# A decoder block with long convolutions on one core: part of the filter transform and five inverse transforms split by steps modulo 4, and two additions moved from TensorE to GpSimd

## The chip, the cores and the metric

The kernel runs on one core of a Trainium2 chip. The metric is the device time of one execution in microseconds, as the median of several executions; lower is better. A profile is one execution taken by the hardware profiler: it records every instruction of the five engines. The text calls them PE (TensorE, matrix multiplication; PEld is its weight loading, which overlaps), DVE (VectorE), ACT (ScalarE), POOL (GpSimd) and SP (SyncE, which only issues transfers here).

## The reference

One decoder block over `x` of shape (4, 1024, 256): a Hyena operator, cross attention to 64 context positions, and a feed-forward layer with ternary weights, each followed by a residual and a layer norm. Everything is float32.

```python
def hyena(u):                                  # per batch, L = 1024, D = 256
    res = depthwise_conv3((u @ w_in.T + b_in).T, conv_w, conv_b)   # 3 * D channels
    x0, x1, v = res.split(3)
    h = hyena_filter(L, D, ...)                # 2 filters per channel, each of length L
    for n in range(2):                         # two orders
        y = irfft(rfft(v, 2 * L) * rfft(h[n], 2 * L))[:L]
        v = y * (x0, x1)[n]
    return v.T @ w_out.T + b_out

x = layernorm(x + hyena(x))
x = layernorm(x + cross_attention(x, ctx))     # 16 heads of 16, 64 keys, output bias b_out
x = layernorm(x + bitlinear_ffn(x))            # 256 -> 1024 gate and up -> 256, quantised activations
```

What matters here is the long convolution, done by matrices in place of a fast transform; the output bias of the attention; and the quantised inner layer, whose rounded values are held with an offset.

## The kernel before

**Long convolution.** The work is cut in eight units: four batches times two halves of 128 channels. A unit runs `stage_j` (three projections with a width-3 convolution, done on ACT and by accumulating transfers that GpSimd issues), `stage_tv` and `stage_tx` (eight 128 x 128 PE transposes each, in `turned`), and then for each of the two orders a data transform `stage_f`, a product with the filter's transform `stage_p`, and an inverse transform `stage_i0` or `stage_i1`. `stage_i1` ends with a multiply by `x1` into `v2s`, and `stage_o` (one for each batch) does the output projection, the residual and the layer norm.

The transforms are plain matrix products against cosine and sine tables `fw` (forward) and `gi_` (inverse), 512 x 512 each. Even and odd steps are already transformed apart: each half needs matrices of half the size, and DVE joins the two results by one sum and one difference (`stage_f`, lines 655 and 656). So a data transform is 16 float32 matmuls of 128 x 128 weights against 256 columns, and so is an inverse transform: for each of four output blocks, four matmuls that sum over cosines and sines (lines 713 and 736). The profile counts a float32 matmul as two passes with a weight load each. In `stage_i0` the table is the weights and the data are the 256 columns; in `stage_i1` the data are the weights and the table the columns.

The filters are transformed once (`filters`, line 523): the eight blocks `hsb` of 128 steps x 512 (two filters, 256 channels) go through 32 matmuls of 512 columns, `ha`, one group of four for each (`dl`, `cs`, `kt`). ACT copies half of each result to `hospace`, DVE writes sum and difference into `hf`, and two large multiply-adds over `hf` finish it. PE, DVE and ACT queue in program order here, with four PSUM buffers of 1024 columns (`big1`).

**From unit 6 on** (line 836) the instructions are not issued as written. `Engines` holds every call as a `Step`; `plan` (line 248) then lists them engine by engine, greedily: among the steps whose inputs are ready, or nearly so within `SLACK`, it takes the one with the lowest rank, which is its place `at` plus an `OFFSET` for its stage. `cost` (line 108) holds the planner's assumed durations. So the last two units, the rest of the convolutions (`rest`, line 874) and the 32 attention and feed-forward tiles of 128 tokens are mixed into one order, which is then kept.

**Attention and feed-forward, per tile.** `att_s` (scores and their maxima on DVE, split into parts on GpSimd), `att_e` (scores again, less the maxima, and the exponential on ACT), `att_v` (values and denominators, on PE with small weights), `att_o` (output projection, residual, norm), `ffn_x` (quantise, transpose), `ffn_h` (gate and up, their product, its maximum, quantise), `ffn_d` (down projection), `ffn_o` (norm and store).

Two details that the change touches. In `att_o`, the output bias enters as a matmul of ones against the bias row `brow` that opens the PSUM sum (line 1162). In `ffn_h`, GpSimd copies the low halves of the rounded values to `h16` (line 1213), which SP's transposing transfer turns to `hT`; these halves carry an offset of 1536 (`HALF`). `ffn_d` sums eight matmuls against `wd_q` and takes the offset out with a ninth, `neg16` against `wd_s`, the sum of the weights (line 1223), which `sum_wd` prepares once on GpSimd (line 1003).

`norm` (line 1148) is statistics on DVE, a reciprocal root by GpSimd's power, and a scaling on DVE.

Of the kernel before, what the change touches and what calls it, by code (L numbers as in the profile page):

```python
# [20 lines left out]
INNER = 1024  # L21
EPS = 1e-5
MAGIC = 12582912.0

# [60 lines left out]
class Step:  # L85
# [22 lines left out]
    def cost(self):  # L108

        n = self.n  # L110
        if self.dma:
            if "transpose" in self.what:
                return 1.25, 2.2
            if self.engine == "POOL":
                return 1.3, 5.0
            return 0.45, 2.0 + self.out.nbytes() / 90e3
        if self.engine == "PE":
            lhs, rhs = self.ins[0], self.ins[1]
            if self.what == "transpose":
                return (0.11 if self.out.dtype == FP else 0.056), 0.2  # L120
            one = 0.002 + rhs.free_size() * (2 if rhs.dtype == FP else 1) / 2400
            one = 2 * max(one, 0.112) if rhs.dtype == FP else one

            return (one / 4 if self.mode else one), 0.2
        if self.engine == "DVE":
            if self.what == "reciprocal" and n > 8:
                return 0.27, 0.17
            if self.what == "scalar_tensor_tensor":
                return 0.065 + n / 900, 0.17
            return 0.065 + n / 960, 0.17  # L130
        if self.engine == "ACT":
            return 0.1 + n * 0.00098, 0.15
        if self.what == "tensor_copy":
            return 0.1 + n * 0.00096, 0.06
        return 0.52 + n * 0.001 * (n > 64), 0.06

# [163 lines left out]
def follow(steps, before, order):  # L300
# [6 lines left out]

SLACK = {"PE": 0.00, "DVE": 0.10, "ACT": 0.72, "POOL": 0.0, "SP": 0.0}
TABLE_RANK = 2.87
OFFSET = dict(  # L310
    att_q=-0.91, att_e=-2.18, att_s=-3.90, att_v=-1.58, att_o=-0.51, ffn_x=-0.32, ffn_h=-1.21, ffn_d=2.05, ffn_o=8.51, rest=-1.48
)
# [3 lines left out]
def decoder_kernel(  # L316
# [81 lines left out]
    def layernorm(r, dst, name):  # L398
# [54 lines left out]
    if True:  # L453
# [69 lines left out]
        def filters():  # L523

            hsb = [spare[4 + t // 2][:, t % 2 * 512 : t % 2 * 512 + 512] for t in range(8)]
            for t in (0, 1, 4, 5, 2, 3, 6, 7):
# [3 lines left out]
                tt_(hsb[t], hsb[t], fdb[:, 1, :], ALU.add)  # L530
            n = 0
            for dl in range(2):
                for cs in range(2):
                    for kt in range(2):
                        m = (2 * cs + kt) * P
                        ha = big1(f"ha{dl}_{cs}_{kt}")
                        for par in range(2):
                            for mt in range(2):
                                mm(
                                    ha[:, par * 512 : par * 512 + 512],  # L540
                                    fw[:, 2 * par + mt, m : m + P],
                                    hsb[4 * par + 2 * dl + mt],
                                    start=mt == 0,
                                    stop=mt == 1,
                                )
                        ho = hospace[:, n % 4]
                        n += 1
                        nc.scalar.copy(ho, ha[:, 512:1024])
                        for st, op in ((0, ALU.add), (1, ALU.subtract)):
                            f = slice(st * 256 + kt * P, st * 256 + kt * P + P)  # L550
                            tt_(
                                hf[:, :, dl, cs, f],
                                ha[:, 0:512].rearrange("p (n d) -> p n d", d=P),
                                ho.rearrange("p (n d) -> p n d", d=P),
                                op,
                            )
            for cs in range(2):
                stt(
                    hf[:, :, 1, cs, :],
                    hf[:, :, 0, 1 - cs, :],  # L560
                    pv[:, C_SG + cs : C_SG + cs + 1],
                    hf[:, :, 1, cs, :],
                    ALU.mult,
                    ALU.add,
                )

# [35 lines left out]
        def turned(u, src, dst, name):  # L602

            ps = big1(f"tr{name}_{u}")
            for par in range(2):
                for j in range(2):
                    for mt in range(2):
                        c, o = (4 * par + 2 * j + mt) * P, (4 * par + 2 * mt + j) * P
                        nc.tensor.transpose(ps[:, o : o + P], src[:, c : c + P], ident)
            nc.scalar.copy(dst, ps)  # L610
# [22 lines left out]
        def stage_f(u, n):  # L633
# [3 lines left out]
            vf = r_vf().rearrange("p (c s f) -> p c s f", c=2, s=2)  # L637
            s["vf"] = vf
            for cs in range(2):
                ps = big1(f"f{u}_{n}_{cs}")  # L640
# [17 lines left out]
        def stage_p(u, n, half):  # L658
# [41 lines left out]
            tt_(q2[:, 0], q1[:, :, 0, :], q1[:, :, 1, :], ALU.add)  # L700
            tt_(q2[:, 1], q1[:, :, 0, :], q1[:, :, 1, :], ALU.subtract)

        def stage_i0(u, *parts):
# [6 lines left out]
            for i in parts or range(4):  # L710
                par, mt = i // 2, i % 2
                o = i * 256
                for m in range(4):
                    mm(
                        ps[:, o : o + 256],
                        gi_[:, m, par * 256 + mt * P : par * 256 + mt * P + P],
                        y[:, par, m // 2, (m % 2) * 256 : (m % 2) * 256 + 256],
                        start=m == 0,
                        stop=m == 3,
                    )  # L720
# [4 lines left out]
        def stage_i1(u):  # L725
# [7 lines left out]
            for par in range(2):  # L733
                for j in range(2):
                    o = (2 * par + j) * 256
                    for m in range(4):
                        c = (m % 2) * 256 + j * P
                        mm(
                            ps[:, o : o + 256],
                            y[:, par, m // 2, c : c + P],  # L740
                            gi_[:, m, par * 256 : par * 256 + 256],
                            start=m == 0,
                            stop=m == 3,
                        )
            tt_(v2s[b][:, dh, :], ps, s["x1"], ALU.mult)

# [252 lines left out]
    r_hT = Ring(*parts(hfree[3][:, 512:2048], 8 * P, F16))  # L999

    wd_s, neg16 = q0h[0][:, 512:640].bitcast(F16), q0h[0][:, 640:704].bitcast(F16)

    def sum_wd():
        nc.gpsimd.memset(neg16, -HALF)
        part = q0h[0][:, 0:512].bitcast(F16)
        w = wd_q.rearrange("p k f -> p (k f)")
        nc.gpsimd.tensor_tensor(part, w[:, 0:1024], w[:, 1024:2048], ALU.add)
        nc.gpsimd.tensor_tensor(part[:, 0:512], part[:, 0:512], part[:, 512:1024], ALU.add)
        nc.gpsimd.tensor_tensor(wd_s, part[:, 0:256], part[:, 256:512], ALU.add)


    kb = {}
# [135 lines left out]
    def norm(r, dst, name):  # L1148
# [6 lines left out]
        nc.gpsimd.tensor_tensor(rs, ve, mhalf[:, 0:1], ALU.pow)  # L1155
        ts_(dst, r, mv[:, 0:1], rs, ALU.subtract, ALU.mult)
# [36 lines left out]
    def ffn_h(g, t):  # L1193
# [61 lines left out]
    while done_d < NT:  # L1255
# [16 lines left out]
        if i == 7:  # L1272
            nc.at, nc.stage = i, "rest"
            sum_wd()
        n = 0 if i < 8 else 2 if i % 4 == 3 else 1
# [18 lines left out]
def _constants():  # L1294
# [9 lines left out]
    even_odd = np.arange(L).reshape(L // 2, 2).T.reshape(L)  # L1304
    t = np.linspace(0.0, 1.0, L, dtype=np.float32)[even_odd]
    bands = np.arange(33, dtype=np.float32)
# [76 lines left out]
```

## Time and profile before

| what | us |
|---|---|
| median of 3 executions | 723.73 |
| lowest and highest of them | 722.44, 726.07 |
| the profiled execution | 723.07 |
| its span, first to last instruction | 721.3 |

| stretch of the span | from | to |
|---|---|---|
| loads, filter basis, first projections | 0 | 33.4 |
| filter transforms (`ha`) | 33.4 | 60.9 |
| convolutions, issued as written | 60.9 | 309.5 |
| planner's order: last convolutions with the first attention tiles | 309.5 | 479 |
| attention with feed-forward | 479 | 690 |
| last tiles run out | 690 | 721.3 |

How to read it: busy time adds up the records of an engine's instructions in a stretch; an engine busy for the whole of it sets its length. Matmuls are pipelined, so a record is longer than the time until the next one starts, and the pace is read from a row of many. The chain of waits goes back from the last instruction, at each step to whatever released it. "issue" is time in which the engine waited for nothing that the profile shows.

### The profile page before, as it was taken

What the parts mean: (1) busy time and instruction counts of PE and PEld (TensorE: products, weight loads), DVE (VectorE), ACT (ScalarE), POOL (GpSimd) and SP (SyncE); (2) the same over time, 40 slices, a digit from 0 to 9 for tenths busy, and PEclk for the clock granted to TensorE, in tenths of its full rate; (3) what the DMA queues carried; (4) which work ended last, traced back from release to release, by engine and by line L of the source; (5) the groups of instructions that cost most, each with busy time, mean ns of one, the idle gap of its engine ahead of it and who ended that gap; (6) DMA issues with size and microseconds to landing.
All of it is one profiled execution on the core that took longest, in us unless ns stands there. A gap on an engine that the chain in (4) does not pass through costs nothing.

```text
span 721.3 us, 12520 instructions
## 1 busy us (share of the span) xinstructions
PE 680.3 (94%) x4920; PEld 472.6 (66%) x4950; DVE 604.2 (84%) x1125; ACT 371.2 (51%) x522; POOL 192.0 (27%) x347
## 2 busy tenths in 40 slices
PE   5999899999999999989999989999999999999973
PEld 2346487878687786867868856866666666566632
DVE  4636759999989999689866986587999898999996
ACT  5512535163461526306322112349898889788861
POOL 1210212012121221214101034123344334343443
PEclk9999999999999999999999999999999999999996
DMA  8853655457370654705830100000222223222133
GB/s 294 169 107 118 141 93 91 84 102 133 59 161 15 140 94 75 129 1 100 185 117 2 58 1 1 2 2 16 53 59 54 53 45 67 39 60 60 38 79 96
DMA packets 65296, 57.61 MB, mean 80 GB/s; under 512 B 38516, under 2 KB 49396, under 8 KB 65238
## 3 DMA queue, kind: packets, MB, share of 16 engines
q0 software_dynamic: 13056, 25.17, 20.6%
q1 hardware_dynamic: 47612, 27.84, 14.8%
q10 hardware_dynamic: 4570, 3.81, 1.8%
q8 instruction: 39, 0.64, 0.4%
q14 instruction: 19, 0.16, 0.1%
HBM read 17.47 MB, written 4.19 MB: 30 GB/s over the span
## 4 chain that ended last, share of the span: by engine, by line
PE 75%; DVE 16%; issue 2%; POOL 2%; DMA 2%; ACT 1%; ACTq 0%; POOLq 0%; DVEq 0%; SPq 0%
PE ps_t L82 37%; PE f L61 12%; PE i L61 10%; PE pj L61 9%; PE ha L61 4%; DVE q L82 3%; DVE small_t L82 3%; PE o L61 2%; DVE x1sp L82 1%; DMA w_in<-in_w_inT 1%; DVE q L61 1%; DVE xt L82 1%; DVE x1sp L61 1%; DVE x1c L82 1%; DVE ln_t L82 1%
## 5 line engine op out<-in xcount | busy, mean ns | idle before, releaser
L82 PE MATMUL ps_t<-hf 128*128 128x256 f16 (+1 forms) x482 | 101.9, 332 | 11.1 <-DMA hf<-vf 3.3
L61 PE MATMUL f<-vt,fw 128*128 128x256 f32 x384 | 84.9, 379 | 1.1 <-ACT vt L61 1.1
L61 POOL DMA_DIRECT2D xc<-tap x28 | 33.9, 1245 | 193.2 <-ACT tap L61 119.5
L82 PEld LDWEIGHTS <-hf 12*128 12x128 bf16 (+2 forms) x768 | 57.5, 99 | 40.4 <-issue 15.7
L61 PEld LDWEIGHTS f<-vt,fw 128*128 128x128 f32 x384 | 72.9, 190 | 13.3 <-issue 2.4
L61 PE MATMUL pj<-xt,w_in 128*128 128x512 f32 x168 | 76.5, 608 | 4.2 <-DMA w_in<-in_w_inT 4.2
L61 PEld LDWEIGHTS pj<-xt,w_in 128*128 128x128 f32 x168 | 32.6, 196 | 42.2 <-issue 41.5
L61 ACT ACTIVATE tap<-pj,tbias,pv 128x1024 f32<-128x1024 f32 x42 | 48.8, 1217 | 11.9 <-DMA xc<-tap 11.9
L61 DVE TENSOR_TENSOR q<-q 128x1024 f32<-128x1024 f32 x44 | 53.0, 1219 | 0.4
L61 DVE TENSOR_TENSOR q<-vf,hf 128x1024 f32<-128x1024 f32 (+1 forms) x33 | 51.8, 1576 | 0.6
L82 DVE TENSOR_REDUCE xt<-ps_t 128x16 f32<-128x1024 f32 x32 | 38.9, 1217 | 14.9 <-PE ps_t L82 13.1
L61 ACT ACTIVATE xc<-pj,cbias,pv 128x512 f32<-128x512 f32 x28 | 20.3, 775 | 58.3 <-PE pj L61 58.3
L82 DVE SCALAR_TENSOR_TENSOR q<-ps_t,small_t,q 128x512 f32<-128x512 f32 x64 | 47.4, 741 | 3.1 <-ACT q L82 1.4
L82 ACT ACTIVATE q<-ps_t,small_t 128x512 f32<-128x512 f32 x64 | 43.9, 685 | 11.3 <-PE ps_t L82 10.3
L61 PE MATMUL i<-q,gi__122 128*128 128x256 f32 x192 | 45.2, 390 | 2.7 <-DVE q L61 2.7
L61 PEld LDWEIGHTS i<-q,gi__122 128*128 128x128 f32 x192 | 37.1, 196 | 10.8 <-DVE q L61 3.5
L61 ACT COPY vo<-f 128x512 f32<-128x512 f32 x24 | 14.1, 586 | 58.2 <-PE f L61 34.0
L82 POOL TENSOR_TENSOR small_t<-small_t,mhalf 128x1 f32<-128x1 f32 x64 | 36.1, 568 | 28.0 <-DVE small_t L82 27.4
L61 DVE TENSOR_TENSOR vf<-f,vo 128x512 f32<-128x512 f32 x48 | 31.1, 683 | 14.2 <-ACT vo L61 14.2
L82 ACT ACTIVATE vf<-q,chalf,small_t 128x1024 f32<-128x1024 f32 x32 | 39.6, 1238 | 6.3 <-DVE small_t L82 4.8
L82 PE MATMUL ps_t<-tap,hf 128*32 128x128 f32 (+1 forms) x896 | 42.3, 261 | 0.4 <-DVE xc L82 0.3
L82 POOL TENSOR_TENSOR xt<-xt 128x16 f32<-128x16 f32 x64 | 18.9, 296 | 83.7 <-DVE xt L82 69.3
(163 smaller groups left out, 1495.1 us busy)
## 6 DMA issues: line engine op xcount, KB each, us to landing
xc<-tap POOLq DMA_DIRECT2D x32, 512.0 KB, 5.1
x1c<-tap POOLq DMA_DIRECT2D x16, 512.0 KB, 7.0
xt<-in_xT SPq DMA_DIRECT2D x8, 512.0 KB, 6.2
x1sp<-in_x SPq DMA_DIRECT2D x8, 512.0 KB, 4.2
out_y<-v SPq DMA_DIRECT2D x32, 128.0 KB, 1.7
hf<-x1sp SPq DMA_DIRECT2D x3, 512.0 KB, 2.9
fw<-in_dftf SPq DMA_DIRECT2D x1, 1024.0 KB, 13.1
gi__122<-in_dfti SPq DMA_DIRECT2D x1, 1024.0 KB, 10.0
```

Of the source, the lines that this page charges most:

```text
L61: return f(*a, **k)
L82: pin(steps[i].f(*steps[i].a, **steps[i].k))
```

## The change

**Steps modulo 4.** A transform over even (or odd) steps can be halved once more, since a cosine over steps 2m takes equal or opposite values at mirrored frequencies. The host orders the steps of all tables, and of the filters' positions, modulo 4, and orders the frequencies of the tables so that frequency k and its mirror stand 256 columns apart (`_constants`). `turned` reads its source at every second element to give the same order, and `stage_i1`'s last multiply writes the natural order back, at stride 2. These hold for all eight units.

The shortened transform itself is used in two places. In `filters`, for the filters of the first kind (`dl` = 0, one half of the work), `fourths` computes only half of the frequencies with 256 columns a matmul, and `join` makes the other half by sums and differences on DVE. For the second kind the matmuls stay as before, and the large multiply-adds become eight small ones. In the inverse transforms named in `FOUR` (order 0 of units 6 and 7, order 1 of units 5, 6 and 7; all in the planner's part), `stage_p` combines mirrored frequencies first with eight more DVE instructions, and each output block then needs two matmuls in place of four (`back`, `stop_of`); in `stage_i1` the blocks are also half as wide. `FOUR` names no data transform, so `stage_f` stays as it was.

**Bias and offset.** The bias row is loaded once to all partitions (`bo`, one more transfer on ACT's queue), and GpSimd adds it to `x1` ahead of the residual add; the matmul of ones goes. GpSimd subtracts the offset while it makes `h16`; the ninth matmul and `sum_wd` go.

**Planner.** Two assumed durations, `SLACK`, `TABLE_RANK` and the offsets get other numbers. `ACTN` is empty, so the new branch in `norm` is not taken.

```diff
+FOUR = {("i", 6, 0), ("i", 7, 0), ("i", 5, 1), ("i", 6, 1), ("i", 7, 1)}
+ACTN = ""
...
-        if self.what == "tensor_copy":
+        if self.what in ("tensor_copy", "tensor_scalar_add"):
             return 0.1 + n * 0.00096, 0.06
+        if n == 16:
+            return 0.22, 0.06
...
-SLACK = {"PE": 0.00, "DVE": 0.10, "ACT": 0.72, "POOL": 0.0, "SP": 0.0}
-TABLE_RANK = 2.87
+SLACK = {"PE": 0.00, "DVE": 0.00, "ACT": 0.67, "POOL": 0.0, "SP": 0.0}
+TABLE_RANK = 1.14
 OFFSET = dict(
-    att_q=-0.91, att_e=-2.18, att_s=-3.90, att_v=-1.58, att_o=-0.51, ffn_x=-0.32, ffn_h=-1.21, ffn_d=2.05, ffn_o=8.51, rest=-1.48
+    att_q=-1.72, att_e=-2.59, att_s=-4.30, att_v=-2.14, att_o=-0.43, ffn_x=-0.54, ffn_h=-1.38, ffn_d=1.90, ffn_o=7.93, rest=-1.58
 )
...
-            for dl in range(2):
-                for cs in range(2):
-                    for kt in range(2):
...
-            for cs in range(2):
-                stt(hf[:, :, 1, cs, :], hf[:, :, 0, 1 - cs, :], pv[:, C_SG + cs : C_SG + cs + 1], hf[:, :, 1, cs, :], ALU.mult, ALU.add)
+            for half in range(2):
+                n2 = slice(2 * half, 2 * half + 2)
+                c2 = slice(256 * half, 256 * half + 256)
+                ps = fourths(f"ha{half}", lambda par, q: hsb[4 * par + q][:, c2])
+                h = hf[:, n2, 0]
+                join(h.rearrange("p n c (s k d) -> p s c k n d", s=2, k=2), h[:, :, :, 0:256], h[:, :, :, 256:512], *ps)
+            for cs in range(2):
+                for kt in range(2):
...
+                    for st, op in ((0, ALU.add), (1, ALU.subtract)):
...
+                        tt_(h1, ha[:, 0:512].rearrange("p (n d) -> p n d", d=P), ho.rearrange("p (n d) -> p n d", d=P), op)
+                        stt(h1, h0, pv[:, sg : sg + 1], h1, ALU.mult, ALU.add)
+        def fourths(name, steps):
+            for q in (1, 0):
+                ps = big1(f"{name}_{q}")
+                for par in range(2):
+                    for cs in range(2):
+                        o = (2 * par + cs) * 256
+                        v = steps(par, q)
+                        mm(ps[:, o : o + 256], fw[:, 2 * par + q, cs * 256 : cs * 256 + P], v, start=True, stop=True)
+                if q:
+                    nc.scalar.copy(pr_t, ps)
+            return ps, pr_t
+        def join(d, e, o, ps0, ps1):
...
+                for st in range(2):
+                    tt_(d[:, st, :, 0], x0[:, st], x1[:, st], ALU.add)
+            tt_(d[:, 0, 0, 1], x0[:, 0, 0], x1[:, 0, 0], ALU.subtract)
+            tt_(d[:, 0, 1, 1], x1[:, 0, 1], x0[:, 0, 1], ALU.subtract)
+            tt_(d[:, 1, 0, 1], x0[:, 1, 1], x1[:, 1, 1], ALU.subtract)
+            tt_(d[:, 1, 1, 1], x0[:, 1, 0], x1[:, 1, 0], ALU.subtract)
+            tt_(e, e, o, ALU.add)
+            for k in range(2 if len(e.shape) == 4 else 1):
+                o1, e1 = (v[:, k] if len(e.shape) == 4 else v for v in (o, e))
+                stt(o1, o1, -2.0, e1, ALU.mult, ALU.add)
...
+            s5 = src.rearrange("p (r j m q) -> p r j q m", r=2, j=2, q=2)
...
-                        nc.tensor.transpose(ps[:, o : o + P], src[:, c : c + P], ident)
+                        nc.tensor.transpose(ps[:, o : o + P], s5[:, par, j, q], ident)
...
+            if ("i", u, n) in FOUR:
+                y = q2.rearrange("p r c (k f) -> p r c k f", k=2)
+                ev, od = y[:, 0], y[:, 1]
+                tt_(ev[:, 0, 0], ev[:, 0, 0], ev[:, 0, 1], ALU.add)
+                stt(ev[:, 0, 1], ev[:, 0, 1], -2.0, ev[:, 0, 0], ALU.mult, ALU.add)
+                tt_(ev[:, 1, 0], ev[:, 1, 0], ev[:, 1, 1], ALU.subtract)
+                stt(ev[:, 1, 1], ev[:, 1, 1], 2.0, ev[:, 1, 0], ALU.mult, ALU.add)
+                for c in range(2):
+                    tt_(od[:, c, 0], od[:, c, 0], od[:, 1 - c, 1], ALU.add)
+                for c in range(2):
+                    stt(od[:, 1 - c, 1], od[:, 1 - c, 1], -2.0, od[:, c, 0], ALU.mult, ALU.add)
+        def back(u, n, par, q):
+            if ("i", u, n) not in FOUR:
+                return [(2 * c + k, (c, k)) for c in range(2) for k in range(2)]
+            return [(2 * c, (1 - c if par and q else c, q)) for c in range(2)]
...
-            tt_(v2s[b][:, dh, :], ps, s["x1"], ALU.mult)
+            natural = "p (a m q) -> p a q m"
+            tt_(
+                v2s[b][:, dh, :].rearrange(natural, a=4, q=2),
+                ps.rearrange("p (a q m) -> p a q m", a=4, q=2),
+                s["x1"].rearrange(natural, a=4, q=2),
+                ALU.mult,
+            )
...
+    bo = tap_t[2][:, 256:512]
+    load_late(bo, rows[1:2, :].to_broadcast([P, D]))
...
-    def sum_wd():
...
-        mm(o, ones16, brow[:, 1, :], start=True, stop=False)
         for kt in range(2):
-            mm(o, cT[:, kt * P : kt * P + P], wo_sb[:, kt, :], start=False, stop=kt == 1)
+            mm(o, cT[:, kt * P : kt * P + P], wo_sb[:, kt, :], start=kt == 0, stop=kt == 1)
         x1 = x1all[g][:, t, :]
+        nc.gpsimd.tensor_tensor(x1, x1, bo, ALU.add)
         tt_(x1, o, x1, ALU.add)
...
-        nc.gpsimd.tensor_copy(h16, low(hq))
+        nc.gpsimd.tensor_scalar_add(h16, low(hq), -HALF)
...
-            mm(po, hT[:, c, :], wd_q[:, c, :], start=c == 0, stop=False)
-        mm(po, neg16, wd_s, start=False, stop=True)
+            mm(po, hT[:, c, :], wd_q[:, c, :], start=c == 0, stop=c == 7)
...
-    n = np.arange(SB).reshape(SB // 2, 2).T.reshape(SB).astype(np.float64)
-    th = np.pi * (2 * np.arange(SB // 2, dtype=np.float64) + 1) / (2 * SB)
+    n = np.arange(SB).reshape(P, 2, 2).transpose(2, 1, 0).reshape(SB).astype(np.float64)
+    k = np.concatenate([np.arange(P), SB // 2 - 1 - np.arange(P)]).astype(np.float64)
+    th = np.pi * (2 * k + 1) / (2 * SB)
```

More of the change, by code (lines that the diff above doesn't have):

```diff
@@ L530, in filters @@
                 tt_(hsb[t], hsb[t], fdb[:, 1, :], ALU.add)
-            n = 0
-            for dl in range(2):
-                for cs in range(2):
-                    for kt in range(2):
[L535 to L555, printed above, removed]
-                            )
@@ L557, in filters @@
-            for cs in range(2):
[L558 to L565, printed above, removed]
+            for half in range(2):
[4 more added lines that the diff above has]
+                join(h.rearrange("p n c (s k d) -> p s c k n d", s=2, k=2), h[:, :, :, 0:256], h[:, :, :, 256:512], *ps)
@@ new lines, in filters @@
+            for cs in range(2):
+                for kt in range(2):
+                    m = (2 * cs + kt) * P
+                    ha = big1(f"ha{cs}_{kt}")
+                    for par in range(2):
+                        for q in range(2):
+                            mm(
+                                ha[:, par * 512 : par * 512 + 512],
+                                fw[:, 2 * par + q, m : m + P],
+                                hsb[4 * par + 2 + q],
+                                start=q == 0,
+                                stop=q == 1,
+                            )
+                    ho = hospace[:, 2 * cs + kt]
+                    nc.scalar.copy(ho, ha[:, 512:1024])
+                    sg = C_SG + (cs + kt) % 2
+                    for st, op in ((0, ALU.add), (1, ALU.subtract)):
+                        f = slice(st * 256 + kt * P, st * 256 + kt * P + P)
+                        h1, h0 = hf[:, :, 1, cs, f], hf[:, :, 0, 1 - cs, f]
+                        tt_(h1, ha[:, 0:512].rearrange("p (n d) -> p n d", d=P), ho.rearrange("p (n d) -> p n d", d=P), op)
+                        stt(h1, h0, pv[:, sg : sg + 1], h1, ALU.mult, ALU.add)
@@ new lines, in fourths @@
+        def fourths(name, steps):
+            for q in (1, 0):
+                ps = big1(f"{name}_{q}")
+                for par in range(2):
+                    for cs in range(2):
[6 more added lines that the diff above has]
+        def join(d, e, o, ps0, ps1):
+            cols = "f" if len(d.shape) == 5 else "n f"
+            n = {} if cols == "f" else {"n": 2}
+            x0, x1 = (v.rearrange(f"p (s c {cols}) -> p s c {cols}", s=2, c=2, **n) for v in (ps0, ps1))
+            if cols == "f":
+                tt_(d[:, :, :, 0], x0, x1, ALU.add)
+            else:
+                for st in range(2):
[8 more added lines that the diff above has]
+                stt(o1, o1, -2.0, e1, ALU.mult, ALU.add)
@@ L604, in turned @@
             ps = big1(f"tr{name}_{u}")
+            s5 = src.rearrange("p (r j m q) -> p r j q m", r=2, j=2, q=2)
             for par in range(2):
                 for j in range(2):
-                    for mt in range(2):
-                        c, o = (4 * par + 2 * j + mt) * P, (4 * par + 2 * mt + j) * P
-                        nc.tensor.transpose(ps[:, o : o + P], src[:, c : c + P], ident)
+                    for q in range(2):
+                        o = (4 * par + 2 * q + j) * P
+                        nc.tensor.transpose(ps[:, o : o + P], s5[:, par, j, q], ident)
             nc.scalar.copy(dst, ps)
@@ L638, in stage_f @@
             s["vf"] = vf
+            if ("f", u, n) in FOUR:
+                ps = fourths(f"f{u}_{n}", lambda par, q: v[:, 4 * par + 2 * q : 4 * par + 2 * q + 2, :])
+                join(vf.rearrange("p c s (k f) -> p s c k f", k=2), vf[:, :, 0, :], vf[:, :, 1, :], *ps)
+                return
             for cs in range(2):
@@ L701, in stage_p, with stop_of @@
             tt_(q2[:, 1], q1[:, :, 0, :], q1[:, :, 1, :], ALU.subtract)
+            if ("i", u, n) in FOUR:
[13 more added lines that the diff above has]
+            return [(2 * c, (1 - c if par and q else c, q)) for c in range(2)]
+        def stop_of(u, n):
+            return 2 if ("i", u, n) in FOUR else 3
         def stage_i0(u, *parts):
@@ L712, in stage_i0 @@
                 o = i * 256
-                for m in range(4):
+                for m, (c, k) in back(u, 0, par, mt):
                     mm(
@@ L716, in stage_i0 @@
                         gi_[:, m, par * 256 + mt * P : par * 256 + mt * P + P],
-                        y[:, par, m // 2, (m % 2) * 256 : (m % 2) * 256 + 256],
+                        y[:, par, c, k * 256 : k * 256 + 256],
                         start=m == 0,
-                        stop=m == 3,
+                        stop=m == stop_of(u, 0),
                     )
@@ L734, in stage_i1 @@
                 for j in range(2):
[L735 to L744, printed above, removed]
-            tt_(v2s[b][:, dh, :], ps, s["x1"], ALU.mult)
+                    for q in range(2):
+                        if q and ("i", u, 1) not in FOUR:
+                            continue
+                        w = P if ("i", u, 1) in FOUR else 256
+                        o = (4 * par + 2 * j + q) * P
+                        for m, (c, k) in back(u, 1, par, q):
+                            mm(
+                                ps[:, o : o + w],
+                                y[:, par, c, k * 256 + j * P : k * 256 + j * P + P],
+                                gi_[:, m, par * 256 + q * P : par * 256 + q * P + w],
+                                start=m == 0,
+                                stop=m == stop_of(u, 1),
+                            )
[5 more added lines that the diff above has]
+                ALU.mult,
+            )
         def stage_o(b):
@@ L999, in decoder_kernel @@
     r_hT = Ring(*parts(hfree[3][:, 512:2048], 8 * P, F16))
-    wd_s, neg16 = q0h[0][:, 512:640].bitcast(F16), q0h[0][:, 640:704].bitcast(F16)
-    def sum_wd():
[L1004 to L1009, printed above, removed]
     kb = {}
@@ L1155, in norm @@
         nc.gpsimd.tensor_tensor(rs, ve, mhalf[:, 0:1], ALU.pow)
-        ts_(dst, r, mv[:, 0:1], rs, ALU.subtract, ALU.mult)
+        if name[0] in ACTN:
+            ts_(ve, mv[:, 0:1], rs, -1.0, ALU.mult, ALU.mult)
+            act(dst, r, AF.Identity, bias=ve, scale=rs)
+        else:
+            ts_(dst, r, mv[:, 0:1], rs, ALU.subtract, ALU.mult)
     def att_o(g, t):
@@ L1271, in decoder_kernel @@
             done_d += 1
-        if i == 7:
-            nc.at, nc.stage = i, "rest"
-            sum_wd()
         n = 0 if i < 8 else 2 if i % 4 == 3 else 1
@@ L1303, in _constants @@
     dfti = (np.concatenate([np.cos(a).T, np.sin(a).T], axis=0) / (SB * L)).astype(np.float32)
-    even_odd = np.arange(L).reshape(L // 2, 2).T.reshape(L)
-    t = np.linspace(0.0, 1.0, L, dtype=np.float32)[even_odd]
+    order = np.arange(L).reshape(2, P, 2, 2).transpose(3, 0, 2, 1).reshape(L)
+    t = np.linspace(0.0, 1.0, L, dtype=np.float32)[order]
     bands = np.arange(33, dtype=np.float32)
```

## The prediction

> **What bounds the kernel now.** I read the page's totals first, then the table of stretches cut where the work changes, then the chain of waits, then single rows. Busy us and share of the span by engine, and the shares of the chain that ended last:
>
> ```profile
> PE 680.3 (94%) x4920; PEld 472.6 (66%) x4950; DVE 604.2 (84%) x1125; ACT 371.2 (51%) x522; POOL 192.0 (27%) x347
> PE 75%; DVE 16%; issue 2%; POOL 2%; DMA 2%; ACT 1%; ACTq 0%; POOLq 0%; DVEq 0%; SPq 0%
> ```
>
> PE leads, but an average hides the stages. By stretch (length, then busy PE, PEld, DVE, ACT, POOL, clock, DMA share, GB/s):
>
> ```profile
> 33.00:61.00 28.00, 28.00 (x68) 12.54 (x68) 14.29 (x20) 5.33 (x9) 2.40 (x2) 1.00 0.51 95
> 100.00:309.50 209.50, 209.10 (x905) 160.89 (x903) 195.93 (x221) 88.76 (x98) 39.30 (x33) 1.00 0.50 93
> 309.50:374.70 65.20, 62.35 (x301) 46.33 (x301) 57.90 (x69) 23.02 (x34) 14.29 (x20) 0.97 0.49 111
> 374.70:434.50 59.80, 54.67 (x458) 41.27 (x458) 49.05 (x83) 10.78 (x22) 12.55 (x14) 0.97 0.06 19
> 434.50:479.00 44.50, 44.45 (x480) 33.46 (x482) 28.79 (x70) 14.44 (x28) 11.91 (x25) 0.96 0.01 1
> 479.00:690.00 211.00, 206.50 (x2447) 134.82 (x2476) 195.84 (x546) 183.17 (x279) 84.16 (x201) 1.00 0.24 49
> ```
>
> The first is the filters: PE solid, DVE half idle. The second is the steady long convolution: PE solid, DVE at 94%. From 309.5 on the planner orders everything: the last convolutions mixed with the first attention tiles (three stretches), then attention with the inner layer (PE 98%, DVE 93%, ACT 87%). A cut on PE pays in full only in the first and the fifth; elsewhere DVE stands close behind.
>
> The prices of matrix work, from the chain (start, us, what):
>
> ```profile
> 33.42 27.47 PE ha L61 x64
> ...
> 100.57 0.87 PE trx L61 x8
> ...
> 104.88 6.91 PE f L61 x32
> ```
>
> A float32 matmul is two passes, so a pass over 512 columns takes 27.47/64 = 0.429 us, over 256 columns 6.91/32 = 0.216, and a float32 transpose over 128 columns 0.87/8 = 0.109.
>
> **The change, part by part.**
>
> *Filters.* The ha work was 64 passes of 512 columns. The half whose steps modulo 4 are apart becomes 2 halves x 2 x 4 matmuls of 256 columns, 32 passes: 32 x 0.216 = 6.9 us; the other half keeps 32 x 0.429 = 13.7. PE: 27.5 - 20.6 = **6.9 us less**. DVE had 16 adds of 512 (0.685 us by their group) and two multiply-adds of 2048 (2.35), about 15 us. Now: two joins, each 2 adds of 512, 4 of 256 (0.41), one of 1024 (1.22) and 2 multiply-adds of 512 (0.74, a row that reads PSUM), 5.7 us; and for the other half 4 x (2 x 0.685 + 2 x 0.74) = 11.4; together 22.8. ACT copies twice 1024 columns (1.02) in place of four times 512 (0.585). DVE is free for it when its last filter input is made, at 36.0, and the first join's matmuls end at 33.4 + 3.5 = 36.9; so DVE ends near 59.8. Its next duty, the first data transform, came at 67.24 and now comes 6.9 earlier, 60.3. The cover is 0.5 us: without it each us of DVE delays the first inverse transform, for which PE waits already, by 1 us. I take -6.9, with -4 as the poor end (3 us of DVE uncovered).
>
> *Five inverse transforms.* Order 0 of the last two units: 32 passes of 256 become 16, 3.46 us less each, 6.9. Order 1 of the last three: 32 passes of 256 stay 32, now of 128 columns and each with its own weights. No row has a full float32 pass of 128. The lower bound is the transpose, 0.109; the upper is 0.216, if the weight load (190 ns in its group, PEld) sets the pace. I take 0.109, since the transpose row is the same shape with a load for every pass: 6.91 - 3.5 = 3.4 each, 10.2; at the other end 0. PE: **17.1 us less, or 6.9**. DVE gets 8 instructions of 256 columns a transform, 4 x 0.41 + 4 x 0.476 = 3.5 us by durations; neighbours overlap by some 0.08 (two adds of 512 take 1.29, not 1.37), hence 3.0; I take 3.1, **15.5 in all**.
>
> Now by stretch. The combinations of three (units 6 and 7, order 0; unit 5, order 1) fall in 309.5 to 374.7: DVE 57.9 + 9.3 = 67.2, more than the stretch's 65.2, while PE loses 6.9. The fourth lands in 374.7 to 434.5, whose chain of waits from 399 to 434 is nearly unbroken DVE work. Over both, DVE would have 49.05 + 57.9 + 12.4 = 119.4 in 125 us: nothing is gained, perhaps 1 us lost. The order 1 transforms of units 6 and 7 run in 434.5 to 479, PE solid, DVE with 15.7 us idle: PE loses 6.8 and DVE gains 3.1, so 6 us come out. Sum: **-5**, between -13 (all PE relief, DVE filled elsewhere) and +4 (passes paced by loads, DVE late).
>
> *Biases.* The output bias leaves PE: 32 bfloat16 passes of 256, 0.11 each (the float32 group behind one starts 0.11 later), 3.5 us; so does the offset's ninth pass of the down projection, 0.107 as half of a 0.216 pass, 3.4. DVE is unchanged. 5.8 of these 6.9 fall in 479 to 690, where PE's 98% meets DVE's 93% and ACT's 87%: at best 5.8, at worst 0; I take half, **-3**. GpSimd gets 32 adds of 128 x 256; its nearest row is below, 0.66 us for float16, so 21 us; it loses the weight sums (2.13 + 1.15 + 0.66 + 0.21 = 4.2). Its 32 float16 copies of 1024 (1.05 each) become subtractions: between the copy and the two-input 2.13; I take 1.1, nearest by its one input. At 2.13 it is 35 us more and 1.1 on the last tile's chain. POOL was busy 84 of 211 us there, so it has room, but not for free:
>
> ```profile
> 447.23 1.41 DVE L82 TENSOR_SCALAR x1c<-x1sp,small_t 128x256 f32<-128x256 f32 x1
> ```
> ```profile
> 447.34 1.15 POOL L82 TENSOR_TENSOR q<-q 128x512 f16<-128x512 f16 x1
> 448.45 0.24 POOL L82 TENSOR_TENSOR small_t<-mw,small_t 128x2 f32<-128x2 f32 x1
> 448.65 0.66 POOL L82 TENSOR_TENSOR q<-q 128x256 f16<-128x256 f16 x1
> ```
>
> A DVE normalisation that takes 0.40 alone took 1.41 while GpSimd added. 64 such stand in the tiles; the new adds take 21 of 400 us, so some 5% of the 64, 3 or 4, wait perhaps 0.5 us more: 2 us, inside the "half" above. Behind each new add on POOL's queue stand the splits of the softmax maxima and the reciprocal roots that DVE's norms need; the add itself is early (its operand is ready tiles ahead). The bias row's load joins ACT's queue after the last tap buffer is free; ACT is busy 23 of 65 us there, so nothing waits. SP's transfers keep their number.
>
> [...]
>
> *Strides.* Transposes now read every second element of their float32 input, and the last multiply of each unit reads and writes at stride 2. No float32 row with a stride exists. Nearest: the float16 transposes that read every second element load in 102 ns, as do contiguous float16 weights. I take 0; the other end is each of 16 x 8 transposes at twice 0.109, +14 us, and eight multiplies at twice 1.22, +9.8.
>
> [...]
>
> **Sum.** -6.9 - 5 - 3 = -15. The profiled execution took 723.07 for its span of 721.3; the median of the three runs is 723.73, 0.7 above. 723.7 - 14.9 = **709 us**.
>
> **The rivals.**
> 1. *Half of it is swallowed by DVE.* The filters pay, the rest returns as DVE waits: 723.7 - 6.9 = 717. For it: 119.4 of 125 us above. Against it: 15.7 idle us in the fifth stretch. The same time comes out if the 128-column passes cost 0.216.
> 2. *PE bounds all of it.* The full 6.9 + 17.1 + 6.9 = 30.9 would give 693; the two stretches before 434, which DVE would fill, keep at least 5 of it: 698. For it: 75% of the chain is PE; against it: DVE at 93 to 95%.
> 3. *Strided reads are slow: slower than before.* 14 us of transposes in a solid PE stretch and 5 multiplies there, 6.1 us, on a DVE at 94%: 709 + 14 + 6 = 729. It decides from about 0.19 us a transpose on. For it: no float32 row clears it; against it: the float16 row.
> That the new path isn't taken is excluded for the named transforms: the order of instructions shows the shorter passes.
>
> **How the numbers follow.** The forecast 0.5, rival 1 0.26, rival 2 0.13, rival 3 0.07, something else (late buffers, the planner's order) 0.04. The forecast's own bounds are 701 (-6.9, -13, -3) to 715 (-4, -5, 0); rival 2 and rival 1 extend the range to 697 and 720. Under 0.5% (3.6 us, about what a measurement of this kernel can tell) is no change: 720.1 to 727.3. Faster: the forecast, rival 2 and most of rival 1, 0.85; same 0.06; slower 0.09.
>
> **What would show it.** The ha passes should end near 54 where they ended at 60.9, with the first inverse transform near 77, not 83.9. Transposes stay at 0.109. The order 1 passes start 0.11 apart; at 0.19 or more rival 1 holds. The last layer norm of the convolutions, which ended at 479, should end near 467; the tail, 31 us, stays. If the stretch after 479 grows, POOL or DVE took the place of PE. A first inverse transform at 80 or later breaks the filter term.

## The result: 2.4% slower

| kernel | median, us | lowest to highest | executions |
|---|---|---|---|
| before | 723.49 | 722.44 to 726.07 | 4 |
| after | 740.77 | 739.73 to 742.52 | 4 |

The kernel before was run again beside the changed one. The ratio is 1.0236, 95% interval 1.0202 to 1.0269: 17.3 us slower, where 15 us faster was forecast. The profiled execution of the changed kernel has a span of 738.8 us. The same two lines of its page as before, busy time by engine and the shares of the chain that ended last:

```profile
PE 663.4 (90%) x4822; PEld 459.9 (62%) x4854; DVE 622.6 (84%) x1181; ACT 371.6 (50%) x520; POOL 277.7 (38%) x375
PE 56%; DVE 17%; POOL 10%; ACT 7%; DMA 5%; issue 4%; ACTq 0%; POOLq 0%; another core or an unknown queue 0%; DVEq 0%
```

PE did lose work, 16.9 us of it. But PE no longer sets the time as it did: its share of the chain fell from 75 to 56%, and POOL, ACT and DMA, 5% of the chain together before, now hold 22%. POOL's busy time grew by 85.7 us. By stretch of the changed kernel, at the cuts used before (columns as there), and the chain's piece for the filters:

```profile
33.00:61.00 28.00, 26.90 (x93) 16.88 (x92) 24.50 (x42) 6.58 (x8) 2.38 (x2) 1.00 0.74 171
...
434.50:479.00 44.50, 42.96 (x499) 31.93 (x496) 37.73 (x92) 16.38 (x29) 15.95 (x31) 0.93 0.01 2
479.00:690.00 211.00, 193.18 (x2295) 122.19 (x2324) 179.94 (x510) 172.56 (x263) 133.19 (x206) 0.99 0.23 47
```
```profile
34.84 20.64 PE ha L64 x64
```

The filters went as forecast: 64 passes in 20.64 us. The attention stretch did not. In the same 211 us PE was busy for 193.2 us (206.5 before), DVE for 179.9 (195.8) and ACT for 172.6 (183.2). All three of the engines that led are less busy at once, so something else holds them up, and the one engine that got busier is POOL, 133.2 us (84.2). What the change gave to POOL, by group of instructions over the whole run (count, busy us, mean ns, then its own idle time and what ended it). The first line is the copy of the kernel before, the other two are the changed kernel's:

```profile
L82 POOL COPY vf<-vf 128x1024 f16<-128x1024 f16 x32 | 33.7, 1054 | 27.6 <-ACT vf L82 22.0 <-issue 3.1 <-POOL small_t L82 2.3
...
L85 POOL TENSOR_SCALAR vf<-vf 128x1024 f16<-128x1024 f16 x32 | 89.4, 2793 | 13.4 <-ACT vf L85 11.0 <-POOL small_t L85 1.1
L85 POOL TENSOR_TENSOR x1sp<-x1sp,tap 128x256 f32<-128x256 f32 x32 | 30.5, 970 | 18.2 <-PE ps_t L85 18.2
```

The offset's subtraction takes 2.79 us, where the copy took 1.05 and the forecast said 1.1; the bias add 0.97 where it said 0.66. How 2.79 us on POOL stop PE can be read from the chain of waits inside the tiles (start, us, what):

```profile
641.66 1.25 ACT vf L85
642.91 0.08 issue
642.99 2.86 POOL vf L85
645.85 0.08 issue
645.93 0.22 POOL xt L85
646.15 0.07 issue
646.22 0.22 POOL xt L85
646.44 0.05 issue
646.49 0.73 PE ps_t L85 x3
```

PE waits here for the two 0.22 us splits of another tile's softmax maxima (`xt`, `att_s`). They have nothing to do with the offset; they stand behind the subtraction in POOL's queue, which itself had to wait for ACT. Of PE's waits, the two groups that matter (total us, times, longest):

```profile
PE ps_t L85 <- POOL xt L85: 21.8, 18, 3.1
PE ps_t L85 <- DMA hf<-vf: 11.2, 5, 3.9
```

In the kernel before, PE waited once for the splits and twice for the transposing transfer:

```profile
PE ps_t L82 <- DMA hf<-vf: 3.3, 2, 1.7
...
PE ps_t L82 <- POOL xt L82: 2.2, 1, 2.2
```

### The profile page after: what moved, and what is told of

Its sections match the earlier page's. It is cut to its first block, busy times and chain, and to the rows that moved or that the text cites. A ratio compares the mean times of both kernels' runs of the same rounds, so it can differ in the third digit from the quotient of the medians.

```text
span 738.8 us, 12415 instructions
## 1 busy us (share of the span) xinstructions
PE 663.4 (90%) x4822; PEld 459.9 (62%) x4854; DVE 622.6 (84%) x1181; ACT 371.6 (50%) x520; POOL 277.7 (38%) x375
## 4 chain that ended last, share of the span: by engine, by line
PE 56%; DVE 17%; POOL 10%; ACT 7%; DMA 5%; issue 4%; ACTq 0%; POOLq 0%; another core or an unknown queue 0%; DVEq 0%
PE ps_t L85 19%; PE f L64 11%; PE i L64 10%; PE pj L64 9%; POOL vf L85 5%; DVE q L85 4%; PE ha L64 3%; DVE small_t L85 2%; POOL xt L85 2%; ACT vf L85 2%; DMA xc<-tap 2%; DMA hf<-vf 2%; DVE x1sp L85 2%; ACT L85 2%; PE o L64 2%
## 5 line engine op out<-in xcount | busy, mean ns | idle before, releaser
L85 PE MATMUL ps_t<-hf 128*128 128x512 bf16 (+1 forms) x480 | 104.1, 334 | 15.7 <-DMA hf<-vf 11.2
L85 POOL TENSOR_SCALAR vf<-vf 128x1024 f16<-128x1024 f16 x32 | 89.4, 2793 | 13.4 <-ACT vf L85 11.0
L85 PE MATMUL ps_t<-tap,hf 128*32 128x128 f32 (+1 forms) x896 | 43.8, 263 | 0.6 <-DVE xc L85 0.6
L64 PEld LDWEIGHTS i<-q,gi__122 128*128 128x128 f32 x192 | 37.2, 197 | 10.7 <-DVE q L64 3.5
```

The source lines that it names most:

```text
L64: return f(*a, **k)
L85: pin(steps[i].f(*steps[i].a, **steps[i].k))
```

## The experiments

The theory, A: GpSimd's subtraction makes everything behind it late. Its rivals: B, the planner's new order is slow by itself; C, VectorE's operations take longer beside GpSimd's work; D, the bias adds do the harm; E, the inverse transforms' additions on VectorE cost more than they save. Further rivals are named with the run that tests them.

One difficulty decides the choice of runs. The planner gives the instructions a new order whenever one operation or one assumed duration changes. So the first runs hold the order: they change only what an instruction does when it is issued, after the planning, or put in one that has the same assumed duration. The kernel before was run again with each set, at medians of 723.1 to 724.1 us.

### Prices changed at held order

**Copy for the subtraction.**

```diff
-        nc.gpsimd.tensor_scalar_add(h16, low(hq), -HALF)
+        nc.gpsimd.tensor_copy(h16, low(hq))
```

> The changed kernel with a plain GpSimd copy of the low halves where it subtracts 1536 (the inner layer's offset stays in, so the output carries it); every engine's order is unchanged. Theory A (the 2.79 us subtraction makes GpSimd late for the transposing DMA and for whatever stands behind it): the copy takes 1.05 us; the chain of waits has 15 pieces of POOL vf, 39.8 us, after 479 us, which would fall to some 16, and other work fills part of the 24 us: 717 to 730 us. Rival B (the new order of the planner's part is slow by itself, whatever GpSimd costs): 736 us or more. [...]

Measured: 714.9 us, 0.989 of the time before (0.987 to 0.991). One instruction form, 32 times, is worth 25.9 us, more than the whole loss. That is 2 us below even theory A's range, and far from B's 736. The copies took 1.04 us, and PE's two waits fell, together by 17.6 us (33.0 to 15.4); the other 8 us were not followed wait by wait:

```profile
PE ps_t L85 <- POOL xt L85: 9.0, 7, 3.1
PE ps_t L85 <- DMA hf<-vf: 6.4, 3, 2.4
```

And where the chain of the changed kernel, between 610 and 660 us, went back and forth between ACT, POOL and PE, the chain of this run has long unbroken PE work:

```profile
609.97 23.48 PE ps_t L85 x254
...
637.04 7.35 PE ps_t L85 x132
```

The same order now beats the kernel before, so B falls as the cause of this loss. VectorE's total went from 622.6 to 619.5 us. These 3.1 us are far too few to make 25.9, so C is not the main cause. (From 479 us on the fall is 4.8 us, 214.8 to 210.1, but the faster run has done more of the work by then, so the totals are compared.)

**Bias adds cut to 8 columns.** The planned instruction is issued with its operands cut to `[:, 0:8]`.

> The changed kernel with the 32 GpSimd bias adds cut to 8 of their 256 columns (the rest of the bias is left out); order unchanged, subtraction as in the changed kernel. The adds take 30.5 us of GpSimd, 0.97 us each, but only one of them stands on the chain after 479 us. Theory A: 735 to 741 us, the adds matter little beside the subtraction. Rival D (the adds are what makes GpSimd late): 728 us or less.

Measured: 731.4 us, 1.012 (1.010 to 1.013). That is 9.3 us, more than theory A allowed and less than D asked. The adds hurt in another place than the subtraction: the last scaling of the convolutions' layer norm starts at 468.7 us instead of 474.7, so 6 us of the 9.3 arise before 479 us. Sixteen of the 32 adds are issued there; they average (30.5 - 11.6)/16 = 1.18 us, the sixteen later ones 0.73.

The trace of the changed kernel shows what the average hides. Nine of the sixteen took 0.72 to 0.78 us and seven took 1.46 to 2.68, and each of the seven ran beside a VectorE operation that reads two operands from SBUF, the on-chip memory (`vf` and `hf`, or `q` and `pr`). Most of those operations were stretched as well: four in a row, of 1024 columns, from 356.8 us on, took 1.74 or 1.75 us each, where the same forms without an add beside them took 1.21 to 1.23. So C has a part in what the bias adds cost: VectorE's total is 617.1 us here, 5.5 less than in the changed kernel.

**Both at once.**

> Both of the above at once (copy for the subtraction, adds cut to 8 columns), order unchanged. Theory A: 2 to 6 us below the copy alone, 713 to 728 us. Rival B: still 730 us or more.

Measured: 712.1 us, 0.987 (0.981 to 0.992). That is 0.9 us below theory A's range. With the copy in place the adds cost 2.8 us, which is not clear of noise, since the executions of this run lie between 710.0 and 719.2 us. GpSimd's two edits together cost 28.7 us at this order (23 to 31 by the interval).

**Latency or queue?** Behind the 1.04 us copy a dummy subtraction is issued whose result nobody reads. The cut shows what is issued; the planner does not see the last line, so the order stays.

```diff
-        nc.gpsimd.tensor_scalar_add(h16, low(hq), -HALF)
+        nc.gpsimd.tensor_copy(h16, low(hq))
+        nc.gpsimd.tensor_scalar_add(scratch, low(hq)[:, 0:640], -HALF)
```

> The changed kernel's order with a 1.05 us copy in the subtraction's place (the offset stays in), and straight behind it on GpSimd a dummy subtraction of 640 columns into unused memory, some 1.75 us, that nothing waits for. GpSimd is then as busy as in the changed kernel, but the copy is done, and the transposing DMA can start, 1.75 us earlier. Theory A1 (the loss is the latency between the activation and the transpose): 715 to 722 us, like the copy alone. Theory A2 (the loss is GpSimd's queue: whatever stands behind the subtraction comes late): 733 to 742 us.

Measured: 736.1 us, 1.016 (1.013 to 1.020). The dummy took 1.82 us, so the pair took 2.86, and POOL's total was 277.4 us against 277.7. PE's waits in this run:

```profile
PE ps_t L85 <- POOL xt L85: 22.6, 18, 3.1
...
PE ps_t L85 <- DMA hf<-vf: 1.7, 1, 1.7
```

The wait for the transfer is gone, since the copy is early. The wait for the splits is all there, since the queue is as long. So at this order 21.2 of the 25.9 us (736.1 - 714.9) are the queue (A2), and about 5 are the latency to the transpose (A1).

**What makes the price?** The subtraction in four forms, by `t % 4`.

> Prices, not time: the changed kernel with the subtraction in four forms, one for each tile of a group (the results are not used): tile 0 subtracts 1024 contiguous 16-bit columns, tile 1 512 contiguous 32-bit columns, tile 2 512 strided 16-bit columns, tile 3 copies 1024 contiguous 16-bit columns. If the stride makes the 2.79 us, tile 0 takes about 1.05 us; if arithmetic on 16-bit columns makes it, tile 0 takes about 2.8, tile 2 about 1.45 and tile 1 some 0.7 to 1.4 us. The copy takes about 1.05 us in either case.

```profile
L85 POOL TENSOR_SCALAR vf<-vf 128x1024 f16<-128x1024 f16 x8 | 22.3, 2788 | 3.6 <-ACT vf L85 3.0 <-POOL small_t L85 0.4
L85 POOL TENSOR_SCALAR vf<-vf 128x512 f32<-128x512 f32 x8 | 12.1, 1517 | 4.9 <-ACT vf L85 3.0 <-POOL xt L85 0.8 <-POOL small_t L85 0.8
L85 POOL TENSOR_SCALAR vf<-vf 128x512 f16<-128x512 f16 x8 | 12.1, 1510 | 7.7 <-ACT vf L85 4.8 <-issue 2.8
L85 POOL COPY vf<-vf 128x1024 f16<-128x1024 f16 x8 | 8.3, 1037 | 7.3 <-ACT vf L85 4.8 <-issue 2.0 <-POOL small_t L85 0.5
```

Contiguous columns cost as much as strided ones (2.79), 32-bit columns as much as 16-bit ones (1.52 and 1.51 for 512). So neither rival of the expectation holds as it stands: the stride makes no price, and neither does the width of 16 bits, since the 32-bit form lies above the 0.7 to 1.4 us expected. Among these forms the operation sets the price: (2788 - 1510)/512 = 2.5 ns a column and 0.23 us fixed, against about 1.0 ns a column for a copy. By this line 640 columns take 1.83; the dummy above took 1.82.

### Parts of the change taken back, planned anew

**Both bias edits taken back:** the ones matmul, the ninth matmul with `sum_wd`, and the copy return.

> The changed kernel with both bias edits taken back (bias by a ones matmul, offset by a ninth matmul as in the kernel before); filters, inverse transforms and the planner's new numbers kept. Theory A: the filters' 5 us stay won and the inverse transforms give 0 to 5 us: 713 to 719 us, faster than both kernels. Rival B (the planner's new numbers, or the inverse transforms themselves, cost the time): 725 us or more.

Measured: 716.2 us, 0.991 (0.989 to 0.992): faster than both kernels.

**The offset edit alone taken back; the bias edit alone taken back.**

> The changed kernel with the offset edit alone taken back (GpSimd copies, a ninth matmul subtracts, the planner orders anew); the output bias stays a GpSimd add. Theory A (nearly all of the loss is the subtraction): the copy alone gave 714.9 us, 32 ninth matmuls at about 0.11 us add 3.5 us of TensorE: 714 to 720 us. Rival D (the bias adds are the larger loss once the planner orders anew): 725 us or more.

> The changed kernel with the bias edit alone taken back (ones matmul, no GpSimd add); the subtraction stays on GpSimd. Theory A: the narrowed adds gave 731.4 us, the ones matmuls cost up to 3 us more: 730 to 737 us. Rival F (the subtraction hurts only together with the adds): 722 us or less.

Measured: 727.0 us, 1.004 (1.001 to 1.007), and 747.3 us, 1.031 (1.025 to 1.037). Neither fell where theory A put it, both some 7 to 10 us above, and 727.0 lies in the range that rival D asked. Against the 716.2 us with both edits taken back, the adds alone cost 10.8 us and the subtraction alone 31.1. So F falls, and the subtraction is the larger loss, against D; but the adds cost more here than at held order, and the sizes can't be trusted: each of these kernels also has an order of its own.

**The old planner's numbers under the same operations, and two more orders of them.** The edits are `SLACK`, `TABLE_RANK` and `OFFSET` as before the change; then `TABLE_RANK` 2.0 with ACT's slack 0.69; then DVE's slack 0.05.

> Both bias edits taken back, filters and inverse transforms kept, with the planner's numbers (slack, table rank, offsets) of the kernel before. Theory A (these numbers are worth little by themselves): 713 to 720 us, within 4 us of 716.2. Rival B (the new numbers are wrong for any kernel without the bias edits): 711 us or less; or they carry the gain: 722 us or more.

> The operations of the kernel with both bias edits taken back (716.2 us) in another order: the planner's table rank 2.0 for 1.14, its slack for ScalarE 0.69 for 0.67. If the order scatters the time by some 8 us, as between the two sets of numbers tried: 716 to 728 us. If the order hardly matters: 714 to 718 us.

> The same operations in a third order: the planner's slack for VectorE 0.05 for 0.00. Scatter: 716 to 728 us; no scatter: 714 to 718 us.

Measured: 724.2 us, 0.998 (0.996 to 1.000); 725.0 us, 1.001 (0.999 to 1.004); 714.3 us, 0.988 (0.983 to 0.992). With 716.2 these are four orders of one set of operations, spread over 10.7 us. For the first of the three, theory A had the difference small and missed by 4 us; 724.2 lies in rival B's second branch, where the new numbers carry the gain. The other two settle that this is scatter: one order lies at 725.0 and one, by a change of 0.05 in one slack, at 714.3 us, which beats both kernels of the change.

**The planner alone.** The kernel before, no operation changed, with the changed kernel's numbers and its price for 16-column GpSimd work.

> The kernel before with no operation changed, planned with the changed kernel's numbers and its price for the 16-column GpSimd operations: another order of the same work. From the four orders of one set of operations tried so far (714.3, 716.2, 724.2 and 725.0 us) a shift of up to 8 us either way is expected: 716 to 732 us. If the changed kernel's order were itself the loss (rival B), 735 us or more.

Measured: 733.7 us, 1.016 (1.012 to 1.019). For the old operations the new numbers cost 10.2 us (733.7 - 723.5), a little over the scatter expected and just short of rival B's bound. For the changed kernel's operations B stays out, since the same order gives 714.9 us there with a cheap subtraction; but an order can be worth as much as an edit.

**True prices for the planner.**

```diff
+        if self.what == "tensor_scalar_add":
+            return 2.79, 0.06
+        if n == 256 and self.what == "tensor_tensor":
+            return 0.97, 0.06
```

> The changed kernel, planned with the measured prices (2.79 us for the subtraction where the planner has 1.08, 0.97 us for the bias add where it has 0.78); all the work is the same. Theory A (the work itself on GpSimd costs the time): 733 us or more. Rival B2 (the planner's wrong price makes the order bad; GpSimd has room at 38%): 725 us or less.

Measured: 733.1 us, 1.013 (1.010 to 1.017), at the lower edge of theory A. The planner assumed 0.1 + 1024 x 0.00096 = 1.08 us for the subtraction. Knowing the price it wins 7.7 us, no more than the orders scatter, and stays 18.2 us above the run with the copy. PE's wait for the splits is only 7.6 us here (4 times), less than the 9.0 of the run with the copy. So where the subtraction hurts belongs to the order: in this one the 18.2 us lie elsewhere, and it was not followed where.

### The parts of the forecast that pay

**Filters alone.** First with the planner's old numbers, but the new price for 16-column work, so in a new order; then with that price taken back too, so that the planned part has exactly the old order.

```diff
-        if n == 16:
-            return 0.22, 0.06
```

> The kernel before with the filters' new transform alone (no five inverse transforms, no bias edits, the planner's old numbers). The first inverse transform started 5.3 us earlier in the changed kernel: if nothing gives it back, 716 to 720 us; if the new order gives it back, 723 us or more. Against the kernel with the five transforms under the same numbers (724.2 us): if these are worth the forecast's 5 us, this one takes 726 us or more; if they cost, 719 us or less.

> The kernel before with the filters' new transform alone (and the new order of the positions it needs), the planner's numbers and prices all as before, so that the planned part has the order of the kernel before on every engine. If the 5.3 us by which the first inverse transform starts earlier are kept to the end: 717 to 719.5 us. If the reads of every second column that come with it cost time later, or the strided reads' transposes do (the forecast's third rival): 721 us or more.

Measured: 730.8 us, 1.009 (1.007 to 1.012), and 715.8 us, 0.990 (0.988 to 0.992). The same operations, 15 us apart, by one assumed duration in the planner: in the first run the new order gave back more than the filters won. At held order the filters win 7.7 us, with the first inverse transform at 77.37 us, 6.6 earlier than before. The time is 1.2 us below the lower end expected, so the loss of the forecast's third rival does not show.

**Filters without the inverse transforms,** with the new planner numbers (`FOUR = set()`, both bias edits taken back).

> Both bias edits taken back (716.2 us), and the five inverse transforms made in the old way as well, so that the filters' new transform and the planner's numbers are left of the change. Theory A (the five inverse transforms win 0 to 5 us): 716 to 721 us. Rival E (their additions on VectorE cost more than the matmuls they save): 714 us or less.

Measured: 726.8 us, 1.004 (1.002 to 1.007). That is above the 716 to 721 expected. Against 716.2 under the same numbers the five inverse transforms win 10.6 us; against 724.2 under the old numbers the kernel with filters alone (730.8) gives 6.6. Rival E's bound is met in neither. But each pair also compares two orders, and orders of one set of operations spread over 10.7 us, so neither the size nor the sign of what these transforms are worth is shown. The filters at the old order reach 715.8 us without them.

**The 64 matmuls.** The kernel before at its own order, the ones matmuls and ninth matmuls not issued.

> The kernel before in its own order with the 32 ones matmuls and the 32 ninth matmuls not issued (output bias and offset are left out; nothing takes their place). What the two bias edits could win at most, were GpSimd's side free. Theory A: TensorE sets the pace of these stages, 64 matmuls at about 0.1 us: 3 to 7 us, 717 to 721 us. Rival G (these matmuls lie in waits for other engines): 722 us or more.

Measured: 720.0 us, 0.995 (0.993 to 0.997): at this order 3.9 us are all that the bias edits could win, were GpSimd free.

## Why the prediction was wrong

*Filters, -6.9.* Right: 64 passes in 20.64 us as worked out, 7.7 us at held order. The `ha` passes ended at 55.5 instead of 54, having started 1.4 us later than before; the first inverse transform started at 78.60, forecast 77, before 83.93.

*Five inverse transforms, -5.* Open. The two pairs give 6.6 and 10.6 us, within the scatter of orders. The passes of order 1 start 0.11 us apart, the price that was taken. PE's total fell by 14.0 us (677.8 to 663.8 in the pair with the new numbers), forecast 17.1; DVE's rose by 9.2 (607.7 to 616.9), forecast 15.5. DVE was charged too much; what that is worth in time is not shown.

*Biases, -3.* This step failed. Its PE side was sound: "half" of 5.8 us against a measured 3.9. Its GpSimd side was "I take 1.1, nearest by its one input", with 2.13 as the other end. The price was 2.79, beyond both ends, and the step from the copy's 1.04 to it is worth 25.9 us at held order. The choice by the number of inputs was a guess that no row supported: the copy's row shows moving, not arithmetic, and the only arithmetic row of that size was the two-input add, which was the nearer one. That row was also a single sample. The very same instruction, `sum_wd`'s first add, 2.13 us in the kernel before, took 2.76 in the kernel with both bias edits taken back:

```profile
L82 POOL TENSOR_TENSOR q<-hf 128x1024 f16<-128x1024 f16 x1 | 2.1, 2126 | 0.0
...
L85 POOL TENSOR_TENSOR q<-hf 128x1024 f16<-128x1024 f16 x1 | 2.8, 2761 | 0.0
```

The consequence was mis-sized as well. At 2.13 the forecast charged "35 us more and 1.1 on the last tile's chain": work, and one latency. The text even named what stands behind each new add on POOL's queue, the splits and the roots, but priced nothing for it, and did not ask what stands behind the longer subtraction. "POOL was busy 84 of 211 us there, so it has room" was the wrong test. The run with the dummy shows what counted here: in GpSimd's queue, one long instruction ahead of a short one that PE waits for is enough (21.2 us for 32 dummies that nothing waits for). At 133 of 211 us POOL still looked far from full.

*At the forecast's own price.* The run with the copy has GpSimd at 1.04 us an offset, about the price that was assumed, and gave 714.9 us: inside the range of 697 to 720 and 6 above 709. So this one price is enough to break the forecast. That the rest came within 6 us is in part luck, since an order alone scatters by 10.7.

*The range.* It was narrower than the text's own terms. The inverse transforms' poor end is given as +4, but the bound of 715 is added up with their -5; with +4 it is 724. That too is below 740.8.

*Strides, 0.* Nearly right. The transposes' weight loads grew from 141 to 206 ns, and they start 0.118 us apart instead of 0.109: 128 x 0.009 = 1.2 us. Rival 3, "slower than before" by strided reads, needed 0.19 and is out. The multiply at stride 2 took 1.226 us, before 1.223.

*The rivals.* None was the mechanism. Rivals 1 and 2 stay on the faster side, rival 3 had the right side for a wrong reason, and the sentence "if the stretch after 479 grows, POOL or DVE took the place of PE" was the one that held: from the last scaling of the convolutions' layer norm to the end it took 264.1 us (474.7 to 738.8), before 242.6 (478.7 to 721.3). That scaling was forecast near 467; with the adds cut it came at 468.7. "The planner's order" got a share of 0.04 with something else; it scatters this kernel's time by over 10 us and deserved a bound of its own in the range.

*The sum, with what was measured.* 723.5 us before; the filters -7.7; the inverse transforms, the 64 matmuls, the new order and what is left of the cheap GpSimd work together -3.7, which is what is left over and can't be told apart better, to reach the 712.1 of the run with GpSimd's two edits made cheap; GpSimd's edits +28.7: 740.8.

## What to carry to other kernels

Work that is moved to a half idle engine is priced by what waits behind it in that engine's queue, and not by the engine's load alone. A rough first price is the added length times how often something on the path stands behind it: here 1.74 us x 18 waits = 31 us, where 25.9 were lost. It was seen in one order only. An operation without a row of its own has no upper bound from a copy of the same size (here 2.79 us against 1.04); measure it in one run, or leave the upper end open. Where a planner sets the order, compare variants at a held order first: here new orders alone moved the time by up to 15 us, as much as the changes under study.

## What the runs showed of the hardware that was not expected

- A one-input subtraction on GpSimd costs 2.5 ns a column, the same for 16 and 32 bits and with or without a stride, 2.7 times a copy of 1024 columns (2.79 and 1.04 us).
- A GpSimd add of 128 x 256 float32 took 0.72 to 0.82 us in 25 of 32 places, and 1.46 to 2.68 us in seven, all beside a VectorE operation on two operands in SBUF. Six such operations of 1024 columns took 1.59 to 1.75 us beside the adds; the same forms without an add beside them took 1.21 to 1.23.
- Transposes that read every second float32 column load their weights in 206 ns instead of 141, yet start only 9 ns later one after the other.
